# Other order at the beginning and between like operations, in a convolution with quantised weights

## The chip, the cores and the metric

One core of one Trainium2 chip. The metric is the device time of one execution in microseconds (us). The kernel before took 1002.18 us, the median of 3 runs (1001.09 to 1002.53). TensorE is called PE here (PEld is its weight load), VectorE DVE, ScalarE ACT, GpSimd POOL, SyncE SP, as in the profile.

## The reference

The input x has 160 images of 128 channels and 32 x 32 pixels. U holds 5 sets of 128 x 128 x 9 weights; image i belongs to the set i % 5 of the reference's order, and the kernel works through them set by set, 32 images each.

```python
beta, alpha = jnp.max(U), jnp.min(U)
s1 = (beta - alpha) / 3.0
v1 = s1 * floor(U / s1)
s2 = s1 / 5.0
v2 = s2 * floor((U - v1) / s2)
w = (v1 + v2).reshape(128 * 5, 128, 3, 3)
# group norm over 32 groups of 4 channels, no scale or shift
z = (x - mean) / sqrt(var + 1e-5)
out = x + conv(z, w, 3x3, padding 1, 5 groups)
```

## The kernel before

**Weights.** `weight_range` finds the range of all U, `Steps.from_range` makes the two step sizes. `make_column` quantises one column of taps (three kernel rows) in 14 small DVE steps (`floor_div`, L108 to L112, `nearest` L99, L125, L453) that a generator gives out one by one; PE turns the result (L462), ACT writes it as `wt` and `half` (L475, L476), and POOL makes the sum and difference taps from it. The three columns of the first set are made at the start (`first`, `second`, `third`). Those of the next set are taken step by step during the images (`take(later, 1)`), from stage 4 of the first set and from the third image of the others, and what is left is run four images before the set ends.

**Statistics.** `measure` gives the sum (L192) and the sum of squares (L199) of one image on ACT, or both on DVE (`st.image`, L182 to L186) where `by_vector` says so. Images go in groups (`cuts`). When a group is measured, PE averages over the channels (`means`, L208), POOL and ACT make deviations, PE averages again (`variances`, L225), and POOL makes `rstd` and `shift` (L235 to L244). Stage i measures ahead up to i + min(10 + i // 2, 15).

**Parts of an image.** A *direct* image (all even ones, and 1, 3, 5) is normalised to z (ACT, L510), rounded to f16 as `hi` (ACT, L518), and the rest of z is `lo` (DVE, L573). From `lo`, `combinations` makes `rows`: differences and sums of pixel rows (L587, L589, L590). A *combined* image (odd, from 7) is combined first (`outer_rows` on POOL, `combine` on DVE, L549 to L555) and then split into `vh` (ACT, L560) and `vl` (DVE, L566).

**Products.** Images 0 to 2 run as plain taps (`direct_hi`, `direct_lo`, L613). From image 3 on, two output rows share products. `sums_of_pairs(i)` puts a sum and a difference part into the PSUM tile `m` (one buffer of two banks). `leave(i)` copies half of m away on ACT (L708), and `pairs(i)` adds and subtracts the two into the tile `eo` (two buffers) on DVE (L717, L718). The remaining products of the image go on top of that (`rest_of_column`, L613 and L650). `residual` multiplies eo by 0.5 into `sum` on ACT (L732), and a POOL DMA adds this to x in SBUF (L745); for images 0 to 2 and the last four a DVE operation does it (L737). SP stores and loads two images at a time.

**The order is written by hand.** No planner moves anything: each engine runs its instructions in the order of the program. Before the loop, `run` writes the start out: statistics of images 0 to 3, ten products of zeros (`warm_up`, L631), the first column, parts of images 0 to 2, then plain taps column by column (the middle one first, `COLS = (1, 0, 2)`). Stage i of the loop then puts PE's `conv(i)` first: `sums_of_pairs(i + 1)`, then the rest of image i in three columns, with a waiting group's `means` in front of the second and `variances` in front of the third column. (In stage 3 the sums come with the second column.) With j = i - 1, ACT's order in a stage is

```python
for k in by_scalar: measure(k, (0,))   # L192
residual(j)                            # L732
leave(i + 1)                           # L708
high_combined(i + 3) or normalise(i + 3), high_part(i + 3)
for k in by_scalar: measure(k, (1,))   # L199
```

and DVE's is `low_combined(i + 2)` or `low_part(i + 2)`, one step of `later`, `combinations(i + 2)` for a direct image, `pairs(i + 1)`, then `combine(i + 4)` or another step of `later`, then measuring on DVE. So an odd stage i multiplies a combined image, writes the sums of a direct one, and normalises a direct one.

Of the kernel before, what the change touches and what calls it, by code (L numbers as in the profile page):

```python
# [132 lines left out]
def run(steps):  # L133

    while True:
        try:
            next(steps)
        except StopIteration as end:
            return end.value
# [170 lines left out]
class Main:  # L310
# [24 lines left out]
    STAT_LEAD = 14  # L335
    LOAD_LEAD = 20
    STEADY = 7
    MEASURED = 20
    EARLY = 8
    FIRST = 3  # L340

# [4 lines left out]
    def __init__(self, tc, ctx, keep, x, u, out):  # L346
        nc = self.nc = tc.nc
        self.imgs, C, self.H, self.W = x.shape
        P = self.P = nc.NUM_PARTITIONS
        assert C == P and self.H * self.W == 1024  # L350
        self.per_set = self.imgs // N_SETS
        self.xv = x.rearrange("(b n) c h w -> n c b (h w)", n=N_SETS)
        self.ov = out.rearrange("(b n) c h w -> n c b (h w)", n=N_SETS)
        self.uv = u.rearrange("n (o i k) -> n o i k", o=C, k=TAPS)

        def pool(name, bufs, **kw):
            return ctx.enter_context(tc.tile_pool(name=name, bufs=bufs, **kw))

        self.const = pool("const", 1)
        self.qpool = pool("quant", 1)  # L360
        self.wpool = pool("weights", 2)
        self.upool = pool("u", 1)
        self.xpool = pool("x", 12)
        self.zpool = pool("z", 3)
        self.parts = pool("parts", 5)
        self.rows = pool("rows", 4)
        self.wide = pool("wide", 1)
        self.wide_parts = pool("wide_parts", 2)
        self.evac = pool("evac", 2)
        self.sums = pool("sums", 4)  # L370
        self.unread = pool("unread", 1)
        self.small = pool("small", 3)
        self.ps_eo = pool("ps_eo", 2, space=PSUM)
        self.ps_m = pool("ps_m", 1, space=PSUM)
        self.ps_stat = pool("ps_stat", 1, space=PSUM)
        self.ps_tr = pool("ps_tr", 1, space=PSUM)
        self.steps = Steps(nc, keep)
        self.chunks, self.z, self.hi, self.v, self.eo, self.m = {}, {}, {}, {}, {}, {}
        self.sum = {}
        self.wts = {}  # L380
        self.columns = []

        cuts = [0, 2, 4, 8, 12, *range(16, self.imgs + 1, 8)]
        self.groups = [range(a, b) for a, b in zip(cuts, cuts[1:])]
        self.group_of = {i: k for k, g in enumerate(self.groups) for i in g}
        self.stats = {}
# [95 lines left out]


    def by_vector(self, i):
        return self.EARLY <= i < self.MEASURED and i % 2 == 0

    def measure(self, i, stages=(0, 1)):

# [91 lines left out]
    def combinations(self, i):  # L580


        nc, P, H, W = self.nc, self.P, self.H, self.W
        lo = self.los[i % len(self.los)]
        rows = self.v[i] = self.rows.tile([P, 2048], MM, tag="rows", name=f"rows{i}")
        d, st = self.halves(rows)
        nc.vector.tensor_sub(d, lo[:, 0:H, :], lo[:, 2 : H + 2, :])  # L587
        pairs = lo[:, 1 : H + 1, :].rearrange("p (i a) w -> p a i w", a=2)
        nc.vector.tensor_add(st[:, 0], pairs[:, 0], pairs[:, 1])  # L589
        nc.vector.tensor_sub(st[:, 1], pairs[:, 1], pairs[:, 0])  # L590

    def halves(self, v):

# [28 lines left out]
    def banks(self, pool, tag, i):  # L622
        return pool.tile([self.P, 2, self.H // 2, self.W], F32, tag=tag, name=f"{tag}{i}")

    def warm_up(self):


        zeros = self.los[3].rearrange("p h w -> p (h w)")
        target = self.banks(self.ps_m, "m", "warm")
        for _ in range(10):  # L630
            self.nc.tensor.matmul(  # L631
                target[:, 0].rearrange("p i w -> p (i w)"), zeros[:, :128], zeros[:, :512],
                start=True, stop=True,
            )

    def direct_hi(self, i, col):
# [39 lines left out]
    def conv(self, i, on_the_way):  # L676


        if self.FIRST < i < self.imgs - 1:
            self.sums_of_pairs(i + 1)  # L680

        for halves in ((0,), (1,)) if i == self.imgs - 1 else ((0, 1),):
            for col in self.COLS:
                if col == self.COLS[1] and i == self.FIRST:
                    self.sums_of_pairs(i + 1)
                if col != self.COLS[0] and halves[-1] == 1:
                    on_the_way(col)
                self.rest_of_column(i, col, halves)
        del self.v[i]
# [18 lines left out]
        self.nc.scalar.copy(m2, self.m[i][:, 1])  # L708
        self.m[i] = self.m[i], m2

    def pairs(self, i):

        nc = self.nc
        m, m2 = self.m.pop(i)
        eo = self.eo[i] = self.banks(self.ps_eo, "eo", i)
        rows = eo.rearrange("p h (i a) w -> p (h i) a w", a=2)
        nc.vector.tensor_add(rows[:, :, 0], m[:, 0], m2)  # L717
        nc.vector.tensor_sub(rows[:, :, 1], m[:, 0], m2)  # L718

    def by_hand(self, i):  # L720
# [33 lines left out]
    def run(self):  # L754
# [39 lines left out]
        def take(steps, count):  # L794
            for _ in range(count):
                next(steps, None)
# [29 lines left out]
        measure(1, 3)  # L826
        self.stats[1].means()
        self.stats[1].deviations()
        self.warm_up()
        parts(0)  # L830
        self.stats[1].variances()
        self.stats[1].deviation()
        self.stats[1].scales()
        self.normalise(1)
        run(first)
        self.high_part(1)
        parts(2)
        take(second, 2)
        self.low_part(0)
        take(second, 2)  # L840
        self.low_part(1)
        take(second, 2)
        self.low_part(2)

        for i in range(self.FIRST):
            self.direct_hi(i, self.COLS[0])
# [5 lines left out]
        self.normalise(3)  # L852
        run(second)
        self.high_part(3)
        self.direct_lo(2, self.COLS[0])
        measure(0, 6, 7)
        measure(1, 6, 7)
        for i in range(self.FIRST):
            self.direct_hi(i, self.COLS[1])
            if i == self.FIRST - 1:  # L860
                run(third)
            self.direct_lo(i, self.COLS[1])
        self.stats[2].means()
        self.stats[2].deviations()
        self.low_part(3)
        self.combinations(3)
        self.steps.choose()
        ready, middle, measured, loaded = [], [], self.EARLY, 6
        later, turned = iter(()), []
        for i in range(self.imgs):  # L870
# [27 lines left out]
            else:  # L898
                j = i - 1
                self.conv(i, on_the_way)  # L900
            ahead = i + min(10 + i // 2, self.STAT_LEAD + 1)
            to_measure = range(measured, min(self.imgs, ahead))
            measured += len(to_measure)
            if n + 1 < N_SETS:
                if b == (2 if n == 0 else 0):
                    self.load_set(n + 1)
                if b == (4 if n == 0 else 2):
                    later = (s for col in self.COLS for s in self.make_column(n + 1, col))
            by_scalar = [k for k in to_measure if not self.by_vector(k)]

            if i < self.FIRST:

                if i == self.FIRST - 1:
                    self.leave(i + 1)
                    self.pairs(i + 1)
                    self.combinations(i + 2)
                self.residual(j)
                if i == self.FIRST - 2:
                    self.low_part(i + 3)
                for k in by_scalar:  # L920
                    self.measure(k, (0,))
                self.normalise(i + 4)
                for k in by_scalar:
                    self.measure(k, (1,))
                self.high_part(i + 4)
            else:

                direct = i + 2 < self.imgs and not self.combined(i + 2)
                if self.combined(i + 2):
                    self.low_combined(i + 2)  # L930
                if direct:
                    self.low_part(i + 2)
                take(later, 1)
                if direct:
                    self.combinations(i + 2)
                if i > self.FIRST and self.by_hand(j):
                    self.residual(j)
                for k in by_scalar:
                    self.measure(k, (0,))
                if i > self.FIRST and not self.by_hand(j):  # L940
                    self.residual(j)
                    self.accumulate(j)
                if self.combined(i + 4):
                    self.outer_rows(i + 4)


                if i + 1 < self.imgs:
                    self.leave(i + 1)
                if self.combined(i + 3):
                    self.high_combined(i + 3)  # L950
                elif self.FIRST + 3 < i + 3 < self.imgs:
                    self.normalise(i + 3)
                    self.high_part(i + 3)
                for k in by_scalar:
                    self.measure(k, (1,))
            for st in middle:
# [8 lines left out]
            if i >= self.FIRST:  # L965

                if i + 1 < self.imgs:
                    self.pairs(i + 1)
                if self.combined(i + 4):
                    self.combine(i + 4)  # L970
                else:
                    take(later, 1)
                if b == self.per_set - 4:
                    run(later)

            middle, ready = ready, []
            for k in to_measure:
                if self.by_vector(k):
                    self.measure(k)
                group = self.group_of[k]  # L980
                if k + 1 == self.groups[group].stop:
                    ready.append(self.stats[group])
# [53 lines left out]
```

## Time and profile before

| | us |
|---|---|
| median of 3 runs | 1002.18 |
| the profiled execution | 1001.74 |
| its span | 1000.0 |
| PE busy | 959.1 (96%) |
| ACT busy | 916.5 (92%) |
| DVE busy | 906.7 (91%) |
| POOL busy | 374.4 (37%) |
| PE waits for DVE's L718, in all | 10.5 |
| PE clock granted, 30 to 36 us | 0.50 |

A row of a timeline gives start, duration, engine, line, operation, tiles and shape; in brackets stands how long the engine was idle before it and what ended that. A row of the waits gives who waited for whom, the total in us, how often, and the longest. "L718" is line 718 of the kernel. Matmuls overlap: the spacing of their starts is their price, not the duration of one. The same holds for ACT and DVE to a smaller degree, where a next operation can start some 0.1 us before the row of the last one ends. This spacing of starts is called the pitch.

### The profile page before, as it was taken

The page shows a single profiled execution, that of the slowest core. Times are in us where ns is not written, and L with a number is a line of the kernel's source. Part 1 is how long each engine was busy: PE and PEld are TensorE (multiplying, and loading weights), DVE is VectorE, ACT ScalarE, POOL GpSimd, SP SyncE. Part 2 cuts the span into 40 slices and gives each one's busy share as a digit, 9 for nine tenths or more (in the row PEclk, how much of TensorE's full clock was granted, in tenths as well). Part 3 has the DMA queues.
Part 4 walks back from the last instruction along what each step waited for, and adds up shares of the span by engine and source line. Part 5 has one row for each costly group of instructions (what it writes and reads, how often), then busy time and mean ns, then how long its engine had stood idle before and what let it go on. Part 6 is the DMA issues. An engine that isn't in the chain of part 4 may idle for free.

```text
span 1000.0 us, 15935 instructions
## 1 busy us (share of the span) xinstructions
PE 959.1 (96%) x5920; PEld 576.2 (58%) x5920; DVE 906.7 (91%) x1227; ACT 916.5 (92%) x1249; POOL 374.4 (37%) x567
## 2 busy tenths in 40 slices
PE   1889999999999999999999999999999999999997
PEld 1445556665666665666666566666665666666554
DVE  7989899999999999989999999999999988888884
ACT  4877999999999999999999999999999999998560
POOL 3523164353515143625243443515243523233310
PEclk9899999999999999999999999999999999999999
DMA  9638789999999999999999999999999999997773
GB/s 365 239 105 232 196 220 262 280 262 274 287 272 264 261 273 265 267 275 281 273 279 263 260 270 269 293 276 277 268 253 264 281 282 262 274 244 196 192 179 141
DMA packets 67287, 254.42 MB, mean 254 GB/s; under 512 B 5248, under 2 KB 5248, under 8 KB 67200
## 3 DMA queue, kind: packets, MB, share of 16 engines
q1 hardware_dynamic: 45168, 173.09, 50.5%
q0 software_dynamic: 22032, 80.23, 41.2%
q8 instruction: 48, 0.79, 0.3%
q14 instruction: 39, 0.32, 0.1%
HBM read 89.19 MB, written 83.89 MB: 173 GB/s over the span
## 4 chain that ended last, share of the span: by engine, by line
PE 82%; DVE 8%; ACT 6%; issue 2%; DMA 1%; POOL 1%; SPq 0%; DVEq 0%; ACTq 0%
PE eo L613 27%; PE m L650 27%; PE eo L650 27%; ACT junk L199 2%; ACT vh L560 1%; ACT sum L732 1%; PE m L613 1%; DVE lo L573 1%; DVE eo L717 1%; DVE eo L718 1%; ACT m L708 1%; ACT z L510 1%; DVE vl L566 1%; DVE st L182 1%; DMA range<-in_L_conv_U_dram 1%
## 5 line engine op out<-in xcount | busy, mean ns | idle before, releaser
L650 PEld LDWEIGHTS <-wt 128*128 128x128 f16 x4212 | 410.8, 98 | 238.5 <-DVE eo L718 9.2
L613 PE MATMUL eo<-hi,wt 128*128 128x496 f16 (+1 forms) x1476 | 355.0, 377 | 4.6 <-DVE eo L718 3.3
L745 POOL DMA_DIRECT2D xt<-sum x153 | 135.9, 888 | 456.2 <-ACT sum L732 440.0
L613 PEld LDWEIGHTS <-wt 128*128 128x128 f16 x1548 | 152.1, 100 | 151.1 <-DVE eo L718 3.8
L566 DVE SCALAR_TENSOR_TENSOR vl<-v,rstd,vh 128x2048 f16<-128x2048 f32 x77 | 180.8, 2347 | 3.1 <-ACT vh L560 3.1
L650 PE MATMUL m<-vh,wt 128*128 128x496 f16 (+1 forms) x462 | 175.5, 380 | 5.9 <-DVE eo L718 5.9
L650 PE MATMUL eo<-vl,wt 128*128 128x256 f16 (+1 forms) x924 | 177.1, 273 | 0.0
L650 PE MATMUL eo<-vh,wt 128*128 128x256 f16 (+1 forms) x924 | 177.1, 273 | 0.0
L199 ACT ACTIVATE junk<-xt,mv 128x1024 f16<-128x1024 f32 x154 | 176.3, 1145 | 0.3
L192 ACT ACTIVATE junk<-xt 128x1024 f16<-128x1024 f32 x154 | 162.7, 1057 | 14.0 <-DMA xt<-in_x_dram 10.9
L650 PE MATMUL m<-vl,wt 128*128 128x496 f16 (+1 forms) x462 | 175.4, 380 | 0.0
L732 ACT ACTIVATE sum<-eo 128x1024 f32<-128x1024 f32 x153 | 154.2, 1008 | 16.6 <-PE eo L650 16.6
L717 DVE TENSOR_TENSOR eo<-m,m 128x512 f32<-128x512 f32 x157 | 109.0, 694 | 61.2 <-ACT m L708 60.8
L560 ACT ACTIVATE vh<-v,rstd 128x2048 f16<-128x2048 f32 x77 | 155.0, 2013 | 0.3 <-DVE v L555 0.3
L650 PE MATMUL eo<-rows,wt 128*128 128x248 f16 (+1 forms) x960 | 144.3, 273 | 0.0
L650 PE MATMUL m<-rows,wt 128*128 128x496 f16 (+1 forms) x480 | 116.9, 380 | 1.4 <-DVE eo L718 1.3
L718 DVE TENSOR_TENSOR eo<-m,m 128x512 f32<-128x512 f32 x157 | 109.8, 699 | 5.4
L708 ACT COPY m<-m 128x512 f32<-128x512 f32 x157 | 91.2, 581 | 25.3 <-PE m L650 22.4
L510 ACT ACTIVATE z<-xt,shift,rstd 128x1024 f32<-128x1024 f32 x83 | 103.2, 1244 | 2.6 <-POOL shift L242 2.6
L573 DVE TENSOR_TENSOR lo<-z,hi 128x1024 f16<-128x1024 f32 x83 | 101.6, 1224 | 1.8 <-ACT hi L518 1.8
L518 ACT CAST hi<-z 128x1024 f16<-128x1024 f32 x83 | 86.8, 1045 | 2.5
L549 DVE TENSOR_TENSOR v<-xt 128x960 f32<-128x960 f32 x77 | 88.5, 1150 | 0.0
(111 smaller groups left out, 824.8 us busy)
## 6 DMA issues: line engine op xcount, KB each, us to landing
xt<-in_x_dram SPq DMA_DIRECT2D x78, 1024.0 KB, 8.9
out_dram<-xt SPq DMA_DIRECT2D x78, 1024.0 KB, 5.1
xt<-sum POOLq DMA_DIRECT2D x153, 512.0 KB, 6.8
range<-in_L_conv_U_dram SPq DMA_DIRECT2D x4, 576.0 KB, 7.1
u<-in_L_conv_U_dram SPq DMA_DIRECT2D x4, 576.0 KB, 11.5
xt<-in_x_dram SPq DMA_DIRECT2D x4, 512.0 KB, 10.5
out_dram<-xt SPq DMA_DIRECT2D x3, 512.0 KB, 2.7
u<-in_L_conv_U_dram SPq DMA_DIRECT2D x2, 288.0 KB, 3.1
```

Of the source, the lines that this page charges most:

```text
L192: self.nc.scalar.activation(junk, image, ACTF.Copy, scale=-1.0 / image.shape[1], accum_out=self.mv[:, j, 0:1],)
L199: self.nc.scalar.activation(junk, image, ACTF.Square, bias=self.mv[:, j, 0:1], accum_out=self.mv[:, j, 1:2],)
L510: nc.scalar.activation(z, self.image(i), ACTF.Identity, bias=st.shift[:, j : j + 1], scale=st.rstd[:, j : j + 1],)
L560: self.nc.scalar.mul(vh, self.v[i], st.rstd[:, j])
L566: self.nc.vector.scalar_tensor_tensor(vl, self.v[i], st.rstd[:, j], self.hi[i], ALU.mult, ALU.subtract)
L573: self.nc.vector.tensor_sub(lo[:, 1 : self.H + 1, :].rearrange("p h w -> p (h w)"), self.z.pop(i), self.hi[i].rearrange("p h w -> p (h w)"),)
L613: nc.tensor.matmul(target[:, h, r0 - h0 : r1 - h0, c0:c1], self.wts[n, col][:, k, :], tile[:, s0 : s0 + r1 - r0, c0 + dw : c1 + dw], start ...
L650: self.nc.tensor.matmul(target[:, :, c0:c1], self.wts[n, col][:, kind, :], source[:, :, c0 + dw : c1 + dw], start=start, stop=stop, skip_g ...
L717: nc.vector.tensor_add(rows[:, :, 0], m[:, 0], m2)
L718: nc.vector.tensor_sub(rows[:, :, 1], m[:, 0], m2)
L732: nc.scalar.mul(self.sum[i], eo, 0.5)
L745: self.nc.gpsimd.dma_start(self.image(i), self.sum.pop(i), accum_op=ALU.add)
```

## The change

- The zeros' products become 14 and then 7 more behind the first column of weights.
- Low part 2 moves from before the first plain taps to behind the second column's making; its products with the first column move from before to after the first taps of the second column.
- In stages 0 to 2 the order of measuring, normalising and low parts changes; image 9 has its squares taken two stages later, and `normalise(6)` moves to stage 3. The sums of image 4 come with the third column of image 3, not the second.
- Measuring runs ahead by 10 + i // 4 images, not 10 + i // 2 (15 at most as before). DVE measures images 8, 10, 11, 14, 17, 20, 23, 26 and 29; before, it measured 8, 10, 12, 14, 16 and 18. The group of images 16 to 23 becomes two groups of 4.
- In the loop, `normalise(i + 3)` stands ahead of `leave(i + 1)` and `high_part(i + 3)` behind it.
- `pairs` runs one other DVE step between L717 and L718: the third row step in even stages, a step of `later` in odd ones.

```diff
@@ -335,7 +335,7 @@
     STAT_LEAD = 14
     LOAD_LEAD = 20
     STEADY = 7
-    MEASURED = 20
+    MEASURED = 32
     EARLY = 8
     FIRST = 3
 
@@ -380,7 +380,7 @@
         self.wts = {}
         self.columns = []
 
-        cuts = [0, 2, 4, 8, 12, *range(16, self.imgs + 1, 8)]
+        cuts = [0, 2, 4, 8, 12, 16, 20, *range(24, self.imgs + 1, 8)]
         self.groups = [range(a, b) for a, b in zip(cuts, cuts[1:])]
         self.group_of = {i: k for k, g in enumerate(self.groups) for i in g}
         self.stats = {}
@@ -482,7 +482,7 @@
 
 
     def by_vector(self, i):
-        return self.EARLY <= i < self.MEASURED and i % 2 == 0
+        return i in (8, 10) or self.EARLY <= i < self.MEASURED and i % 3 == 2
 
     def measure(self, i, stages=(0, 1)):
 
@@ -584,10 +584,10 @@
         lo = self.los[i % len(self.los)]
         rows = self.v[i] = self.rows.tile([P, 2048], MM, tag="rows", name=f"rows{i}")
         d, st = self.halves(rows)
-        nc.vector.tensor_sub(d, lo[:, 0:H, :], lo[:, 2 : H + 2, :])
+        yield nc.vector.tensor_sub(d, lo[:, 0:H, :], lo[:, 2 : H + 2, :])
         pairs = lo[:, 1 : H + 1, :].rearrange("p (i a) w -> p a i w", a=2)
-        nc.vector.tensor_add(st[:, 0], pairs[:, 0], pairs[:, 1])
-        nc.vector.tensor_sub(st[:, 1], pairs[:, 1], pairs[:, 0])
+        yield nc.vector.tensor_add(st[:, 0], pairs[:, 0], pairs[:, 1])
+        yield nc.vector.tensor_sub(st[:, 1], pairs[:, 1], pairs[:, 0])
 
     def halves(self, v):
 
@@ -622,15 +622,16 @@
     def banks(self, pool, tag, i):
         return pool.tile([self.P, 2, self.H // 2, self.W], F32, tag=tag, name=f"{tag}{i}")
 
-    def warm_up(self):
+    def warm_up(self, count):
 
 
         zeros = self.los[3].rearrange("p h w -> p (h w)")
-        target = self.banks(self.ps_m, "m", "warm")
-        for _ in range(10):
+        if "warm" not in self.m:
+            self.m["warm"] = self.banks(self.ps_m, "m", "warm")
+        for _ in range(count):
             self.nc.tensor.matmul(
-                target[:, 0].rearrange("p i w -> p (i w)"), zeros[:, :128], zeros[:, :512],
-                start=True, stop=True,
+                self.m["warm"][:, 0].rearrange("p i w -> p (i w)"), zeros[:, :128],
+                zeros[:, :512], start=True, stop=True,
             )
 
     def direct_hi(self, i, col):
@@ -681,7 +682,7 @@
 
         for halves in ((0,), (1,)) if i == self.imgs - 1 else ((0, 1),):
             for col in self.COLS:
-                if col == self.COLS[1] and i == self.FIRST:
+                if col == self.COLS[2] and i == self.FIRST:
                     self.sums_of_pairs(i + 1)
                 if col != self.COLS[0] and halves[-1] == 1:
                     on_the_way(col)
@@ -708,13 +709,15 @@
         self.nc.scalar.copy(m2, self.m[i][:, 1])
         self.m[i] = self.m[i], m2
 
-    def pairs(self, i):
+    def pairs(self, i, between=lambda: None):
+
 
         nc = self.nc
         m, m2 = self.m.pop(i)
         eo = self.eo[i] = self.banks(self.ps_eo, "eo", i)
         rows = eo.rearrange("p h (i a) w -> p (h i) a w", a=2)
         nc.vector.tensor_add(rows[:, :, 0], m[:, 0], m2)
+        between()
         nc.vector.tensor_sub(rows[:, :, 1], m[:, 0], m2)
 
     def by_hand(self, i):
@@ -826,21 +829,20 @@
         measure(1, 3)
         self.stats[1].means()
         self.stats[1].deviations()
-        self.warm_up()
+        self.warm_up(14)
         parts(0)
         self.stats[1].variances()
         self.stats[1].deviation()
         self.stats[1].scales()
         self.normalise(1)
         run(first)
+        self.warm_up(7)
         self.high_part(1)
         parts(2)
         take(second, 2)
         self.low_part(0)
         take(second, 2)
         self.low_part(1)
-        take(second, 2)
-        self.low_part(2)
 
         for i in range(self.FIRST):
             self.direct_hi(i, self.COLS[0])
@@ -852,18 +854,20 @@
         self.normalise(3)
         run(second)
         self.high_part(3)
-        self.direct_lo(2, self.COLS[0])
+        self.low_part(2)
         measure(0, 6, 7)
         measure(1, 6, 7)
         for i in range(self.FIRST):
             self.direct_hi(i, self.COLS[1])
+            if i == 1:
+                self.direct_lo(2, self.COLS[0])
             if i == self.FIRST - 1:
                 run(third)
             self.direct_lo(i, self.COLS[1])
         self.stats[2].means()
         self.stats[2].deviations()
         self.low_part(3)
-        self.combinations(3)
+        run(self.combinations(3))
         self.steps.choose()
         ready, middle, measured, loaded = [], [], self.EARLY, 6
         later, turned = iter(()), []
@@ -898,7 +902,7 @@
             else:
                 j = i - 1
                 self.conv(i, on_the_way)
-            ahead = i + min(10 + i // 2, self.STAT_LEAD + 1)
+            ahead = i + min(10 + i // 4, self.STAT_LEAD + 1)
             to_measure = range(measured, min(self.imgs, ahead))
             measured += len(to_measure)
             if n + 1 < N_SETS:
@@ -907,32 +911,35 @@
                 if b == (4 if n == 0 else 2):
                     later = (s for col in self.COLS for s in self.make_column(n + 1, col))
             by_scalar = [k for k in to_measure if not self.by_vector(k)]
+            by_vector = [k for k in to_measure if self.by_vector(k)]
 
             if i < self.FIRST:
 
-                if i == self.FIRST - 1:
-                    self.leave(i + 1)
-                    self.pairs(i + 1)
-                    self.combinations(i + 2)
+                if i == 0:
+                    measure(0, *by_vector, 9)
+                    self.normalise(4)
+                    self.high_part(4)
+                if i == 2:
+                    self.leave(3)
+                    self.normalise(5)
+                    measure(1, 9)
+                    self.high_part(5)
+                    self.pairs(3)
+                    self.low_part(4)
+                    run(self.combinations(4))
                 self.residual(j)
-                if i == self.FIRST - 2:
-                    self.low_part(i + 3)
-                for k in by_scalar:
-                    self.measure(k, (0,))
-                self.normalise(i + 4)
-                for k in by_scalar:
-                    self.measure(k, (1,))
-                self.high_part(i + 4)
+                if i > 0:
+                    measure(0, *by_vector)
             else:
 
-                direct = i + 2 < self.imgs and not self.combined(i + 2)
+                rows = iter(())
                 if self.combined(i + 2):
                     self.low_combined(i + 2)
-                if direct:
+                elif i + 2 < self.imgs:
                     self.low_part(i + 2)
-                take(later, 1)
-                if direct:
-                    self.combinations(i + 2)
+                    take(later, 1)
+                    rows = self.combinations(i + 2)
+                    take(rows, 2)
                 if i > self.FIRST and self.by_hand(j):
                     self.residual(j)
                 for k in by_scalar:
@@ -944,13 +951,15 @@
                     self.outer_rows(i + 4)
 
 
+                part = i + 3 < self.imgs and not self.combined(i + 3)
+                if part:
+                    self.normalise(i + 3)
                 if i + 1 < self.imgs:
                     self.leave(i + 1)
+                if part:
+                    self.high_part(i + 3)
                 if self.combined(i + 3):
                     self.high_combined(i + 3)
-                elif self.FIRST + 3 < i + 3 < self.imgs:
-                    self.normalise(i + 3)
-                    self.high_part(i + 3)
                 for k in by_scalar:
                     self.measure(k, (1,))
             for st in middle:
@@ -965,7 +974,8 @@
             if i >= self.FIRST:
 
                 if i + 1 < self.imgs:
-                    self.pairs(i + 1)
+                    self.pairs(i + 1, lambda: take(rows if i % 2 == 0 else later, 1))
+                run(rows)
                 if self.combined(i + 4):
                     self.combine(i + 4)
                 else:
@@ -974,9 +984,9 @@
                     run(later)
 
             middle, ready = ready, []
+            if i >= self.FIRST:
+                measure(0, *by_vector)
             for k in to_measure:
-                if self.by_vector(k):
-                    self.measure(k)
                 group = self.group_of[k]
                 if k + 1 == self.groups[group].stop:
                     ready.append(self.stats[group])
```

## The prediction

> **What bounds the kernel now.** I read the table of engines first, then the busy time by stretches, then who waits for whom, then the timeline of one steady pair of images.
>
> ```profile
> PE 959.1 (96%) x5920; PEld 576.2 (58%) x5920; DVE 906.7 (91%) x1227; ACT 916.5 (92%) x1249; POOL 374.4 (37%) x567
> ...
> 300.00:400.00 100.00, 100.00 (x629) 60.86 (x628) 95.34 (x128) 98.93 (x136) 38.34 (x60) 1.00 0.99 266
> ```
>
> PE is busy 959 of 1000 us, and from 300 to 400 us (second line: PE, PEld, DVE, ACT, POOL busy) 100 of 100, with ACT at 98.9. So after the beginning only PE counts, and what the change can win is PE's idle time: 41 us, of which 17.9 pass before its first product and some 7 after its last. The waits of PE:
>
> ```profile
> PE m L650 <- DVE eo L718: 7.2, 5, 2.0
> ...
> PE eo L613 <- DVE eo L718: 3.3, 1, 3.3
> ```
>
> These 10.5 us (at 59, 69, 95, 121, 147 and 231 us) are the prize. All are waits for the second half of `pairs`. Now one odd (combined) image in the steady state:
>
> ```profile
> 509.52 1.46 PE L650 MATMUL m<-rows,wt 128*128 128x512 f16 x6
> 513.45 0.38 PE L650 MATMUL m<-vh,wt 128*128 128x512 f16 x1
> ...
> 510.38 1.01 ACT L732 ACTIVATE sum<-eo 128x1024 f32<-128x1024 f32 x1
> 511.29 0.58 ACT L708 COPY m<-m 128x512 f32<-128x512 f32 x1
> 511.75 1.25 ACT L510 ACTIVATE z<-xt,shift,rstd 128x1024 f32<-128x1024 f32 x1
> 513.04 1.04 ACT L518 CAST hi<-z 128x1024 f16<-128x1024 f32 x1
> ...
> 510.60 0.60 DVE L110 SCALAR_TENSOR_TENSOR tt<-tt,s1r,nn 128x384 f32<-128x384 f32 x1
> 511.90 0.70 DVE L717 TENSOR_TENSOR eo<-m,m 128x512 f32<-128x512 f32 x1 [0.69 <-ACT m L708]
> 512.63 0.70 DVE L718 TENSOR_TENSOR eo<-m,m 128x512 f32<-128x512 f32 x1
> ```
>
> PE starts the sums of the next image at 509.52 (call it T0) and, 3.93 us later, the sums of the one after. Those write the only m buffer, so they need L718 to be over: 512.63 + 0.70 = 513.33, 0.12 us before PE arrives at 513.45. **There is almost no slack here**, though PE never waits. From the rows: the copy L708 starts at 511.29, L717 0.61 later, L718 0.73 later, and PE can go on 0.76 after that, as its waits show (the row below at 148.49, for an L718 at 147.73). So the next sums start no earlier than copy + 2.10 us.
>
> ```profile
> 148.49 0.39 PE L650 MATMUL m<-vh,wt 128*128 128x512 f16 x1 [1.30 <-DVE eo L718]
> ```
>
> The copy comes behind `sum` (L732) in ACT's order, and `sum` reads the eo whose last product ends after T0. Where ACT waited for it, it started 0.20 us after PE's next sums could have started (69.17, against 68.53 + 4 x 0.109 = 68.97). So the copy must start by T0 + 3.93 - 2.10 = T0 + 1.83. Today it can: the sums are done at about T0 + 1.5, `sum` lets ACT go at T0 + 0.2 + 0.91 = T0 + 1.11.
>
> **The change, part by part.**
>
> *Zeros.* The clock is 0.50 from 29.7 to 36.5 us; 14 of the first 18 weight products there are 0.43 apart instead of 0.21, so warm ones save 14 x 0.21 = 3.0 us. 11 more zeros cost 4 x 0.21 before the wait for POOL at 28.34 (hidden by it: the ten end at 27.18) and 7 x 0.21 from 28.95 to 30.45, just as the first weights (L475) come; nothing on the path. But what is late next is ACT:
>
> ```profile
> 39.85 1.23 ACT L510 ACTIVATE z<-xt,shift,rstd 128x1024 f32<-128x1024 f32 x1
> 40.99 0.47 ACT L475 ACTIVATE wt<-pt 128x384 f16<-128x384 f32 x1
> ```
>
> The second column of weights is written at 40.99 because ACT is in one unbroken row of statistics and normalising from 32.3 us, none of which is moved. PE stood at this wait already (41.51). So I cost the zeros at nothing. If the clock turned late and all 14 took 0.43, they would end at 29.5, 1.2 us past the wait that hides them, and the second statistics with them; that is the bound on the other side. The Trainium skill (TensorE: Matmul & The Clock Gate, Part 1) says the clock doubles after about 3.4 us of busy window and falls after an idle one; the rows agree (0.50 for 6.8 us), and by the rule alone the change would win the 3.0 us.
>
> *Low part 2, its products and its place.* Six products (1.27 us) go from before this wait into the stretch after it, where PE has no idle time until 59 us: +1.27 there. The 1.22 us on DVE only changes its place.
>
> *Images 0 to 2.* `measure(8)` now fills DVE's wait at 50.5, low part 4 comes after `pairs(3)`. Adding rows: residual(0) ends at 57.7, measure(10) takes 1.68, so L717 starts at 59.4, L718 at 60.1, and image 3 starts at 60.9 instead of 62.4: -1.5 us.
>
> *A new wait.* Image 11 is now measured on DVE (11 % 3 is 2), behind `pairs(3)` (1.34), low part 4 (1.23), three row steps (1.28), a residual (1.14) and its own 1.75: ready at 66.15. The group's means product stands in PE's order behind image 3's first column, at 62.6. Everything of PE is queued behind it: +3.6 us. With `leave(4)` after sums moved one column on, image 4's stage begins at 71.65 (70.43 today): +1.2.
>
> *Lead and measuring.* ACT gets 9 images instead of 12 up to stage 11 (2.4 us each), which removes ACT's lateness behind the 1.92, 2.03 and 1.30 us stalls in stages 7, 11 and 15. DVE gets 17, 20, 23, 26, 29 later (1.69 each), of which I take 0.45 each into PE by the DVE slack of about 1.2 in that stage (bounds 0 and 1.69).
>
> *Normalise ahead of leave; a step between L717 and L718.* These hold for the whole run. `normalise(i+3)` exists for odd i only (i+3 is even, not combined): exactly the tight stage. It is one ACT instruction, no DMA. The copy now starts at T0 + 0.20 + 0.91 + 1.15 (z's pitch to an independent follower, 54.75 to 55.90) = T0 + 2.26, past the 1.83. Between L717 and L718 comes one step of the next set's weights: L717's pitch is then 0.61 (as L718 to L549: 512.63 to 513.24), the step's on average 0.47 (0.27 to 0.67 by rows), instead of 0.73: +0.35. So the next sums start at T0 + 2.26 + 0.61 + 0.61 + 0.47 + 0.76 = T0 + 4.71, PE waits 4.71 - 3.93 = **0.78 us per pair**; where no set is being prepared, T0 + 2.26 + 2.10 = 4.36, **0.43 us**. In even stages PE's rest is 5.1 us long and all this is hidden. The gains of this edit are hidden too: z to hi 1.29 to 1.15 on ACT, 0.12 on DVE. [...]
>
> **The sum**, against the profiled execution (1001.74 us, span 1000.0; 0.44 under the median shown). Up to stage 7: +1.1 (the +1.2 of image 4, carried on). Stages 7 to 18: six odd stages x 0.78 + 5 x 0.45 - 5.25 (today's stalls), so +2.8 in all at stage 19. From stage 19 to 155 there are 69 odd stages; 44 of them have weight steps (5 in the first set, 13 in each of three): 44 x 0.78 = 34.3; 25 x 0.43 = 10.8. Today's stall at 231 goes: -0.6. At stage 21 normalise(24) may wait for POOL's shift, one stage after its statistics (POOL's L235 took 2.98): +1.5 (0 to 3). Statistics and turn products, some 0.15 each, that PE does inside the new waits: -3.3. Together +45.5: **1047 us**.
>
> **Rivals.**
> *Faster.* PE keeps its 100% because ACT, with 7 us less to do early, runs ahead, so that in odd stages the copy starts by T0 + 1.83. Then only the stalls at 95, 121, 147 and 231 go: -5.9, 996 us. For it: these stalls are ACT's and DVE's lateness, and both get relief. Against: `sum` cannot start before the product it reads, however early ACT is. It decides at 0.43 us.
> *Half the price.* The step between falls beside something, and every odd stage costs 0.43: 69 x 0.43 = 30 and +0.1 for the rest: 1032. For it: in four of ten odd stages that is the case already.
> *Twice the price.* ACT does not come back to T0 + 0.20 but stays 0.66 late as at 510.38: 44 x 1.44 + 25 x 1.09 = 91: 1092. For it: ACT is 98.9% busy. Against: the pair gets 0.78 longer and ACT's work doesn't.
> *No effect.* Costs and gains cancel, if the copy lands at 1.83 by shorter pitches.
>
> **How the numbers follow.** Forecast (1036 to 1058, by pitches 0.15 either way over 69 stages and the early bounds) 0.74; half the price 0.10; twice 0.06; faster 0.08; no effect 0.02. Range 1026 to 1062: forecast and half price, 0.84. A measurement tells about 0.2% from no change; slower by more than that 0.90, within it 0.02, faster 0.08.
>
> **What would show it.** Right: PE's table has "PE m L650 <- DVE eo L718" some 70 times with 0.4 to 0.8 us; PE below 96% at 300 to 400; in an odd stage ACT's order is sum, z, m, hi, sum follows a PE wait. The zeros: clock 1.00 at 30 to 36 us and a wait for L475 at 41.5 that is longer (39.0 to 41.5). The new wait: L208 waits for image 11's statistics near 62 to 66 us. Wrong: if PE is at 100% after 300 us, the odd stage was misread and the start alone decides.

## The result, and the profile after

The changed kernel takes **1050.26 us** (median of 6 runs, 1048.43 to 1051.16) where the kernel before took 1001.65 beside it: a ratio of 1.0482, 95% interval 1.0469 to 1.0496. The prediction was 1047 us in a range of 1026 to 1062. The profiled execution took 1050.74 us, its span is 1049.0.

The table of engines and the stretch from 300 to 400 us (busy us of PE, PEld, DVE, ACT, POOL) of the changed kernel:

```profile
PE 977.0 (93%) x5935; PEld 573.0 (55%) x5935; DVE 896.0 (85%) x1242; ACT 910.9 (87%) x1239; POOL 404.0 (39%) x575
...
300.00:400.00 100.00, 95.58 (x594) 56.79 (x592) 87.75 (x120) 93.84 (x129) 42.18 (x56) 1.00 0.94 255
```

The stretch carries it: 594 matmuls in 100 us, against 629 before, and no engine is full any more. All of PE, DVE and ACT have idle time at once, so this is a chain from engine to engine and not an engine's load. The waits of PE, over the whole run:

```profile
PE m L651 <- DVE eo L721: 34.9, 70, 2.8
...
PE pg L208 <- DVE mv L186: 3.5, 1, 3.5
PE eo L613 <- ACT wt L475: 2.6, 1, 2.6
```

(L651, L719, L721, L709 and L735 are the kernel before's L650, L717, L718, L708 and L732.) In this row, 70 waits for the second half of `pairs` have taken the place of 5. One odd stage, image for image the one shown for the kernel before, from the timelines of PE, ACT and DVE:

```profile
536.00 0.60 PE L651 MATMUL m<-rows,wt 128*128 128x512 f16 x2
540.74 0.39 PE L651 MATMUL m<-vh,wt 128*128 128x512 f16 x1 [0.65 <-DVE eo L721]
...
536.20 1.02 ACT L735 ACTIVATE sum<-eo 128x1024 f32<-128x1024 f32 x1 [0.15 <-PE eo L651]
537.12 1.23 ACT L510 ACTIVATE z<-xt,shift,rstd 128x1024 f32<-128x1024 f32 x1
538.25 0.57 ACT L709 COPY m<-m 128x512 f32<-128x512 f32 x1
538.72 1.05 ACT L518 CAST hi<-z 128x1024 f16<-128x1024 f32 x1
...
538.86 0.70 DVE L719 TENSOR_TENSOR eo<-m,m 128x512 f32<-128x512 f32 x1 [1.02 <-ACT m L709]
539.47 0.61 DVE L110 SCALAR_TENSOR_TENSOR tt<-tt,s1r,nn 128x384 f32<-128x384 f32 x1
540.00 0.69 DVE L721 TENSOR_TENSOR eo<-m,m 128x512 f32<-128x512 f32 x1
```

T0 is 536.00. `sum` now waits for PE and starts at T0 + 0.20; z stands between it and the copy, which starts at T0 + 2.25; L719 follows 0.61 later, the weight step L110 0.61 after that, L721 0.53 after that, and PE goes on 0.74 later, at T0 + 4.74. Before it was T0 + 3.93.

Stage by stage (the start of `sums_of_pairs`, from PE's timeline):

| stretch | before, us | after, us | difference | the prediction's |
|---|---|---|---|---|
| up to stage 4 | 70.4 | 75.8 | +5.4 | +1.2 |
| stages 4 to 18 | 97.6 | 96.6 | -1.0 | +1.6 |
| stages 19 to the end's last sums | 814.5 | 859.1 | +44.6 | +42.7 |

### The profile page after: what moved, and what is told of

Same layout as the page of the kernel before. It is cut to its first block, busy times and chain, and to the rows that moved or that the text cites. A ratio compares the mean times of both kernels' runs of the same rounds, so it can differ in the third digit from the quotient of the medians.

```text
span 1049.0 us, 15983 instructions
## 1 busy us (share of the span) xinstructions
PE 977.0 (93%) x5935; PEld 573.0 (55%) x5935; DVE 896.0 (85%) x1242; ACT 910.9 (87%) x1239; POOL 404.0 (39%) x575
## 4 chain that ended last, share of the span: by engine, by line
PE 57%; ACT 21%; DVE 18%; issue 2%; POOL 1%; DMA 1%; SPq 0%; DVEq 0%; POOLq 0%
PE eo L613 27%; PE m L651 19%; PE eo L651 10%; ACT z L510 7%; ACT sum L735 7%; DVE eo L719 5%; DVE eo L721 5%; ACT m L709 4%; ACT junk L199 1%; DVE vl L566 1%; ACT vh L560 1%; ACT junk L192 1%; PE m L613 1%; DMA range<-in_L_conv_U_dram 1%; DVE st L182 1%
## 5 line engine op out<-in xcount | busy, mean ns | idle before, releaser
L651 PEld LDWEIGHTS <-wt 128*128 128x128 f16 x4212 | 406.4, 98 | 286.8 <-DVE eo L721 57.8
L719 DVE TENSOR_TENSOR eo<-m,m 128x512 f32<-128x512 f32 x157 | 109.0, 694 | 126.2 <-ACT m L709 126.1
L651 PE MATMUL m<-vh,wt 128*128 128x496 f16 (+1 forms) x462 | 177.1, 383 | 34.8 <-DVE eo L721 34.0
L735 ACT ACTIVATE sum<-eo 128x1024 f32<-128x1024 f32 x153 | 155.7, 1018 | 39.8 <-PE eo L651 39.8
L651 PE MATMUL eo<-vl,wt 128*128 128x256 f16 (+1 forms) x924 | 177.1, 273 | 0.0
L651 PE MATMUL eo<-vh,wt 128*128 128x256 f16 (+1 forms) x924 | 177.1, 273 | 0.0
L651 PE MATMUL m<-vl,wt 128*128 128x496 f16 (+1 forms) x462 | 176.4, 382 | 0.0
L199 ACT ACTIVATE junk<-xt,mv 128x1024 f16<-128x1024 f32 x151 | 173.3, 1147 | 0.3
L192 ACT ACTIVATE junk<-xt 128x1024 f16<-128x1024 f32 x151 | 159.8, 1058 | 14.7 <-DMA xt<-in_x_dram 11.6
L651 PE MATMUL eo<-rows,wt 128*128 128x248 f16 (+1 forms) x960 | 144.8, 274 | 0.0
L709 ACT COPY m<-m 128x512 f32<-128x512 f32 x157 | 91.3, 581 | 55.0 <-PE m L651 53.2
L651 PE MATMUL m<-rows,wt 128*128 128x496 f16 (+1 forms) x480 | 117.7, 382 | 0.9 <-DVE eo L721 0.8
L721 DVE TENSOR_TENSOR eo<-m,m 128x512 f32<-128x512 f32 x157 | 108.6, 691 | 1.0
```

What stands on the lines that cost most here:

```text
L192: self.nc.scalar.activation(junk, image, ACTF.Copy, scale=-1.0 / image.shape[1], accum_out=self.mv[:, j, 0:1],)
L199: self.nc.scalar.activation(junk, image, ACTF.Square, bias=self.mv[:, j, 0:1], accum_out=self.mv[:, j, 1:2],)
L651: self.nc.tensor.matmul(target[:, :, c0:c1], self.wts[n, col][:, kind, :], source[:, :, c0 + dw : c1 + dw], start=start, stop=stop, skip_g ...
L735: nc.scalar.mul(self.sum[i], eo, 0.5)
```

## The experiments

Each kernel was timed in turns with the kernel before on the same chip; the kernel before gave 1002.0 to 1002.6 us in these.

**Which edits cost it.** Four kernels divide the change. `start_only` is the changed kernel with

```diff
-                if part:
-                    self.normalise(i + 3)
                 if i + 1 < self.imgs:
                     self.leave(i + 1)
                 if part:
+                    self.normalise(i + 3)
                     self.high_part(i + 3)
...
-                    self.pairs(i + 1, lambda: take(rows if i % 2 == 0 else later, 1))
+                    self.pairs(i + 1)
```

and the steps of `rows` and `later` back in front of `pairs`.

> The changed kernel with the two edits of the steady stages undone: normalise stands behind leave again, and nothing stands between L717 and L718. Theory (the order in odd stages holds PE): the odd stages are 3.93 us again, so 1004 us (999 to 1010): the start's own cost of some 5 us less the early stalls. Rival (the new measuring and lead leave ACT and DVE late for the whole run): most of the 48 us stays, over 1030.

Measured: 1007.82 us (ratio 1.0050, 1.0036 to 1.0063). About 5 of the 48 us belong to all the other edits together. In the profiled execution (1005.56 us, one of the shorter ones) few of them are the start's: from PE's first product to stage 4 it takes 1.3 us more than the kernel before, stages 4 to 18 take 1.3 less, and stages 19 to 30 take 2.2 more (1.7 of it in stage 21); 0.8 us is a later first product. The rival that ACT and DVE stay late for the whole run falls: from stage 31 on the odd stages take 3.92 to 4.24 us again (once 4.78), as in the kernel before (3.92 to 4.23).

`norm_only` is the kernel before with normalise ahead of leave, as in the first diff read backwards; `step_only` is the kernel before with the step between alone; `steady_only` has both.

> The kernel before with one edit: normalise(i + 3) ahead of leave(i + 1). Theory: odd stages of 4.35 us in place of 3.93 to 4.07 over the whole run, 1029 us (1024 to 1036). Rival (the step between alone is to blame): within 3 us of the kernel before. Rival (the start is to blame): the same.

> The kernel before with one edit: another DVE step between the two halves of pairs. Theory: the copy still starts at T0 + 1.52 to 1.8, so only the longer steps stick out, by up to 0.2 us in some stages: 1006 us (1002 to 1012). Rival (the step between alone is to blame): 1030 and more.

> The kernel before with both edits of the steady stages and its own start. Theory: 50 odd stages x 0.78 and 25 x 0.42, less today's stalls: 1044 us (1038 to 1052). If the two add up, this is norm_only and step_only together less 1002; the theory has it above that sum, since the step sticks out fully only behind the later copy.

| kernel | median, us | ratio | interval | odd stages from 31 on, us |
|---|---|---|---|---|
| norm_only | 1028.67 | 1.0261 | 1.0243 to 1.0278 | 4.34 to 4.36, once 4.47 |
| step_only | 1007.49 | 1.0049 | 1.0032 to 1.0065 | 3.92 to 4.27, once 4.88 |
| steady_only | 1046.91 | 1.0443 | 1.0426 to 1.0460 | 4.35 to 4.87 |
| changed kernel | 1050.26 | 1.0482 | 1.0469 to 1.0496 | 4.35 to 4.87 |

All three came as the theory had them. Alone, normalise costs 26 us and the step 5; together they cost 44, 13 more than the sum. That fits the reason given beforehand, that the step's length sticks out fully only where the copy is already late. With the 5 of the other edits this is the whole change. How norm_only looks on ACT, in a stage with T0 = 510.69:

```profile
510.89 1.02 ACT L732 ACTIVATE sum<-eo 128x1024 f32<-128x1024 f32 x1 [0.47 <-PE eo L650]
511.81 1.23 ACT L510 ACTIVATE z<-xt,shift,rstd 128x1024 f32<-128x1024 f32 x1
512.94 0.57 ACT L708 COPY m<-m 128x512 f32<-128x512 f32 x1
```

The copy is at T0 + 2.25 and ACT idles in front of `sum`: it has time, but in the wrong place.

**A double dose.** `norm_hi_ahead` is the kernel before with (`part` is true for the same images as the `elif` of before)

```diff
+                if part:
+                    self.normalise(i + 3)
+                    self.high_part(i + 3)
                 if i + 1 < self.imgs:
                     self.leave(i + 1)
...
-                elif self.FIRST + 3 < i + 3 < self.imgs:
-                    self.normalise(i + 3)
-                    self.high_part(i + 3)
```

> A double dose: the kernel before with normalise(i + 3) and high_part(i + 3) both ahead of leave(i + 1). ACT does the same work. Theory: the copy starts at T0 + 0.20 + 0.91 + 1.28 + 0.95 = T0 + 3.34, the next sums 2.10 later, so odd stages of 5.44 us and 1110 us (1100 to 1116). Rival (a swap on ACT costs what it costs in pipe gaps, not in the place of the copy): about what normalise alone cost, 1025 to 1035.

Measured: 1109.10 us (1.1065, 1.1048 to 1.1082). Every odd stage from 15 to 155 takes 5.43 to 5.45 us; the theory says 5.44. ACT and PE, T0 = 544.24:

```profile
544.45 1.02 ACT L732 ACTIVATE sum<-eo 128x1024 f32<-128x1024 f32 x1 [0.47 <-PE eo L650]
545.37 1.23 ACT L510 ACTIVATE z<-xt,shift,rstd 128x1024 f32<-128x1024 f32 x1
546.63 1.04 ACT L518 CAST hi<-z 128x1024 f16<-128x1024 f32 x1
547.58 0.58 ACT L708 COPY m<-m 128x512 f32<-128x512 f32 x1
...
549.68 0.39 PE L650 MATMUL m<-vh,wt 128*128 128x512 f16 x1 [1.04 <-DVE eo L718]
```

Copy at T0 + 3.34, next sums 2.10 later. With the same work on ACT, 107 us hang on the place of one 0.58 us copy.

**The other side of sum.** `norm_ahead_of_sum` moves normalise one place further up.

```diff
+                if part:
+                    self.normalise(i + 3)
                 if i > self.FIRST and not self.by_hand(j):
                     self.residual(j)
...
-                elif self.FIRST + 3 < i + 3 < self.imgs:
-                    self.normalise(i + 3)
+                elif part:
                     self.high_part(i + 3)
```

> The kernel before with normalise(i + 3) one place further up still, ahead of sum as well. It is then done while ACT waits for the product, and no longer between sum and the copy. Theory: odd stages of 3.93 us again, 1001 us (999 to 1004), since z to hi also costs ACT 0.13 us less per pair. Rival (any normalise ahead of leave costs its 1.15 us): 1028 as with normalise between sum and leave.

Measured: 1005.41 us (1.0033, 1.0022 to 1.0044): 4 us worse than forecast, but not the 1028 of the rival. The stretch from 300 to 400 us is full again:

```profile
300.00:400.00 100.00, 99.99 (x631) 60.65 (x629) 95.07 (x128) 98.27 (x137) 45.40 (x59) 1.00 0.99 270
```

Most of what stays is in stages 9 and 13 (5.19 and 6.12 us where the kernel before has 4.06 and 4.09). In stage 9 ACT comes late from measuring and waits for nobody, and z in front of the copy delays it further. In stage 13 it is z that has to wait, for POOL's shift, and `sum` and the copy stand behind it:

```profile
133.07 1.24 ACT L510 ACTIVATE z<-xt,shift,rstd 128x1024 f32<-128x1024 f32 x1 [2.23 <-POOL shift L242]
```

So "ahead of sum" is free only for an ACT that waits at sum and has its shift already. `lead_and_norm`, the same on top of `lead_only` below, asked whether less early measuring cures that.

> lead_only with normalise(i + 3) ahead of sum. Ahead of sum it made 1005.4 of 1002.0, by odd stages up to 17 in which ACT was late already; from then on the odd stages were 3.92. Theory: with the slower lead ACT is less late, so at most half of the 3.4 us remains: 1001.5 us (1000 to 1003). Rival (normalise ahead of leave costs for good): 1004 and more.

Measured: 1003.25 us (1.0009, 0.9997 to 1.0021), 2.5 above lead_only: a little over the forecast's range; early stages are still paid (5.19 and 5.91 us in stages 13 and 15, against 4.67 and 5.21 in lead_only). No version with normalise ahead of leave paid.

**The zeros.** `zeros_only` is the kernel before with

```diff
-        self.warm_up()
+        self.warm_up(14)
...
         run(first)
+        self.warm_up(7)
```

> The kernel before with 14 and 7 products of zeros in place of 10. Theory: the clock stays at 1.00 from 30 to 36 us, and PE waits longer for the second column's weights at 41.5, so 1002 us (1000.5 to 1003). Rival (the rule of the clock gate alone): the 3.0 us are won, 999.

Measured: 1001.94 us (0.9999, 0.9990 to 1.0008). The clock does stay up; the last column but two of these rows is the granted clock, from 30 to 36 us, first in the kernel before, then in zeros_only:

```profile
30.00:32.00 2.00, 1.51 (x4) 0.58 (x5) 1.97 (x3) 1.75 (x4) 1.92 (x2) 0.50 1.03 412
32.00:34.00 2.00, 2.00 (x6) 0.76 (x5) 1.97 (x4) 1.68 (x2) 1.92 (x4) 0.50 1.02 406
34.00:36.00 2.00, 2.00 (x7) 0.70 (x5) 1.73 (x2) 1.97 (x4) 2.00 (x3) 0.50 1.03 412
```

```profile
30.00:32.00 2.00, 2.00 (x11) 0.89 (x10) 1.70 (x4) 2.00 (x4) 1.84 (x5) 1.00 1.02 406
32.00:34.00 2.00, 1.21 (x7) 0.48 (x5) 1.96 (x4) 1.97 (x3) 2.00 (x3) 1.00 1.04 414
34.00:36.00 2.00, 2.00 (x12) 0.89 (x10) 1.97 (x4) 1.97 (x5) 0.45 (x1) 1.00 1.02 408
```

and the 3 us are given back, most of them in waits for hi of image 2 (0.8), for the second column's k (1.0) and for its L475 (some 0.3), which ACT reaches when it did before, and 0.6 because the first plain tap comes later, 13.2 us behind PE's first product and not 12.6. The fourteen zeros make that delay:

```profile
22.53 5.72 PE L633 MATMUL mwarm<-lo 128*128 128x512 f16 x14
28.55 1.67 PE L633 MATMUL mwarm<-lo 128*128 128x512 f16 x7
```

They take 5.55 us up to the next product, 0.40 each, where the seven later ones lie 0.23 apart. So most of them run at the slow pace, although the clock in this profile reads 1.00 from 16 to 39 us: that reading does not show the slow pace there. The clock stays up afterwards, as forecast, and that is worth nothing here.

**The start.** `start_11_act` and `start_lo2_back` each take one wait out of start_only.

```diff
-        return i in (8, 10) or self.EARLY <= i < self.MEASURED and i % 3 == 2
+        return i in (8, 10) or 12 <= i < self.MEASURED and i % 3 == 2
...
-                    measure(1, 9)
+                    measure(0, 11)
+                    measure(1, 9, 11)
```

> start_only (the new start without the edits of the steady stages) with image 11 measured on ACT, which idles there, not on DVE. Theory: PE's means product no longer waits 3.5 us for DVE: 1004 us (1002 to 1006), against 1007.8 of start_only. If the clock's fall behind this wait costs too, the gain is up to 5 us. Rival (the wait was covered by the later wait for the copy of image 4): under 1 us of gain.

Measured: 1002.19 us (1.0003, 0.9994 to 1.0012): 5.6 below start_only by the medians, 4.7 by the ratios, the most that the forecast allowed. From PE's first product to stage 4 it takes 50.6 us, 1.9 less than the kernel before; stages 19 to 30 take 2.2 more and give that back. `start_only` waits for this image with the whole of PE's queue behind it:

```profile
66.97 0.35 PE L208 MATMUL pg<-mv,gavg 128*128 128x4 f32 x2 [3.48 <-DVE mv L186]
```

`start_lo2_back` puts `low_part(2)` and `direct_lo(2, COLS[0])` back to their old lines.

> start_only with low part 2 and its six products back in their old places. Theory: the products fill PE's 2.6 us wait for the second column again and no longer stand in the full stretch behind it: 1.3 us less than start_only, 1006.5 us, and more where the wait of 2.6 us let the clock fall. Rival (PE's later wait of 3.5 us for image 11 takes all of it back): no change, 1007.8.

Measured: 1005.98 us (1.0038, 1.0024 to 1.0052). The direction is right (-1.8), but the interval overlaps that of start_only, whose runs spread from 1004.3 to 1009.2; this one is not settled. Its profiled execution has a fall of the clock behind the 3.5 us wait for image 11 that it keeps.

`lead_only` is the kernel before with only

```diff
-    MEASURED = 20
+    MEASURED = 32
...
-        cuts = [0, 2, 4, 8, 12, *range(16, self.imgs + 1, 8)]
+        cuts = [*range(0, 4, 2), *range(4, 32, 4), *range(32, self.imgs + 1, 8)]
...
-        return self.EARLY <= i < self.MEASURED and i % 2 == 0
+        return i in (8, 10) or 12 <= i < self.MEASURED and i % 4 == 2
...
-            ahead = i + min(10 + i // 2, self.STAT_LEAD + 1)
+            ahead = i + min(10 + i // 4, self.STAT_LEAD + 1)
```

> The kernel before with the slower lead alone: 10 + i // 4, groups of 4 up to image 31, DVE measures 8, 10, 14, 18, 22, 26 and 30. Image 11 stays on ACT, so PE's means product waits for nobody new. Theory: the stalls of stages 7, 11 and 15 (5.25 us) and at 231 us (0.6) go, at most: 997 us (996 to 1000). Rival (DVE's queue was late there, not ACT's): 1000 to 1003.

Measured: 1000.74 us (0.9987, 0.9978 to 0.9996). Faster, but 3.7 short of the forecast, and inside the range of the rival that DVE's queue was late. From 75 us on, the kernel before, then lead_only:

```profile
PE m L650 <- DVE eo L718: 5.9, 4, 2.0
```

```profile
PE m L650 <- DVE eo L718: 3.9, 6, 1.1
```

The stalls of stages 7 and 11 went (4.06 and 3.93 us in place of 6.01 and 6.26), that of stage 15 hardly (5.21 for 5.39), that of stage 29 not at all (4.86 for 4.88), and smaller ones came in stages 9, 13, 19 and 21 (4.6 to 5.1 us). The traces show both engines behind them. L717 follows the copy by 0.61 us where it waits for it; in stages 9, 15 and 19 of lead_only it follows by 1.6 to 2.2 us, as DVE is still at other work (stage 15 below). In stages 13 and 21 ACT is late: `sum` starts 1.7 and 2.1 us after T0, behind a measurement.

```profile
140.57 0.58 ACT L708 COPY m<-m 128x512 f32<-128x512 f32 x1 [0.27 <-PE m L650]
142.79 0.69 DVE L717 TENSOR_TENSOR eo<-m,m 128x512 f32<-128x512 f32 x1
```

Stage 7 of the kernel before was DVE's as well, and not ACT's as the prediction has it: ACT itself waits for PE there, and L717 comes 3.0 us after the copy.

```profile
93.15 0.59 ACT L708 COPY m<-m 128x512 f32<-128x512 f32 x1 [0.52 <-PE m L650]
96.18 0.69 DVE L717 TENSOR_TENSOR eo<-m,m 128x512 f32<-128x512 f32 x1
```

Only 2.0 of the 5.9 us were won for good.

`start_mended` joins several of these: start_11_act with image 11's sum taken in stage 0, low part 2 in its old place, the sums of image 4 with the second column again, and lead_only's groups and by_vector.

> The new start with its own waits removed: image 11 on ACT (its sum in stage 0, its squares in stage 2), low part 2 in its old place, the sums of image 4 with the second column again, groups of 4 up to image 31 and DVE measuring 8, 10, 14, 18, 22, 26 and 30; the steady stages as in the kernel before. Theory: the stalls at 59 and 69 us (4.6) go or shrink beside those that lead_only takes: 997 us (995 to 1000). Rival (another wait of the start takes their place): 1000 and more.

Measured: **997.42 us** (0.9957, 0.9943 to 0.9970), 4.6 us faster than the kernel before it was timed with, and some 53 less than the changed one takes. In its profile, PE's first product to stage 4 takes 3.6 us less than in the kernel before, stages 4 to 18 take 3.1 less and stages 19 to 30 take 2.1 more; which of the joined edits makes how much of that was not tried. Its first 75 us have no wait of PE for DVE's pairs over 0.5 us, where the kernel before had 3.3 and 1.3:

```profile
PE pg L225 <- POOL dv L222: 2.5, 2, 2.1
PE pt L462 <- DVE k L112: 1.5, 1, 1.5
PE m L613 <- ACT hi L518: 0.8, 1, 0.8
PE eo L613 <- DVE eo L721: 0.5, 1, 0.5
PE m L651 <- DVE eo L721: 0.3, 1, 0.3
```

## Why the prediction was right

**The odd stage: right, in mechanism and in size.** Forecast 4.36 us without a weight step, measured 4.34 or 4.35 in 24 of 25 (stage 29 took 5.08); with a step 4.71 on average, measured 4.48 to 4.87, mean 4.69 (stages from 23 on). The rival "faster" fails where the prediction said it would: `sum` starts at T0 + 0.20 and not sooner, with ACT idle ahead of it. "Half the price" and "twice the price" fail by the means; ACT came back to T0 + 0.20, as its idle time shows (at `sum` it waits for PE 77 times, 39.8 us in all; before, 9 times and 16.6 us).

**The new wait for image 11: right** (3.5 us where 3.6 were forecast), and so was the worth of the zeros (nothing). The reading beside it, that the rows agree with a fall of the clock behind an idle window, does not hold: in the 3.4 us before the fall at 29.7 us PE had waited 1.15 us once and was some 0.5 us into its next wait.

**Stage 21: in its bounds.** It took 6.91 us, some 2.2 over the stages around it, where 1.5 (0 to 3) were given for a wait for POOL. That wait is about half of it; the rest is `sum`, which starts 1.44 us after T0 (184.98), behind a measurement.

```profile
188.53 1.24 ACT L510 ACTIVATE z<-xt,shift,rstd 128x1024 f32<-128x1024 f32 x1 [1.10 <-POOL shift L242]
```

The stall at 231 us (stage 29), which the sum lets go for -0.6, stayed: 4.88 us before, 4.87 in start_only, 5.08 in the changed kernel.

**The start: too cheap by 4.2 us.** What failed is that the sum up to image 4 had no price for the clock. In the profiled execution it was down at 42.3 to 45.7 and at 69.6 to 73.0 us, behind the very waits (2.6 and 3.5 us) that the change makes or lengthens; the products there took 1.7 us more each time, and this execution began 0.7 later. The rest of that sum was right, as start_only shows: its profiled execution has the same two waits and no fall of the clock. Stage 4 begins so in the kernel before, start_only and the changed kernel:

```profile
70.43 1.47 PE L650 MATMUL m<-rows,wt 128*128 128x512 f16 x6 [1.29 <-DVE eo L718]
72.49 1.47 PE L651 MATMUL m<-rows,wt 128*128 128x512 f16 x6 [0.43 <-DVE eo L721]
75.81 1.47 PE L651 MATMUL m<-rows,wt 128*128 128x512 f16 x6 [0.43 <-DVE eo L721]
```

Counted from PE's first product (at 17.89, 18.68 and 18.61 us) these are 52.5, 53.8 and 57.2 us: +1.3 without the falls of the clock, where +1.2 was forecast. The last column but two of these rows is the granted clock in the changed kernel:

```profile
42.00:44.00 2.00, 1.76 (x5) 0.70 (x6) 1.82 (x4) 2.00 (x4) 1.28 (x3) 0.58 0.03 8
44.00:46.00 2.00, 2.00 (x7) 0.68 (x5) 1.89 (x4) 1.94 (x5) 1.31 (x2) 0.56 0.55 145
```

**Stages 4 to 18: too dear by 2.6 us.** Two terms were mis-sized, in opposite directions. The relief of ACT and the extra measuring were to give -3.0 together (-5.25 and 5 x 0.45); in start_only, which has both and not the steady edits, these stages take 96.3 us against 97.6, so only -1.3. The steady edits were to cost 6 x 0.78 = 4.7 there; from start_only to the changed kernel these stages grow by 0.3, and the six odd ones (7 to 17) take 28.1 us in both. They were longer than 3.93 us already (4.06 to 5.20 in start_only), so the price of an undisturbed stage did not come on top. The changed kernel enters stage 4 later, which may help it here; that was not tried.

**The sum** was 45.5 us over the kernel before's own profiled time; the profiled execution after was 49.0 over it. Of the 3.5 missing, 4.2 are the start's, -2.6 the next stages', 1.9 the rest, most of it the clock after stage 21 (stage 22 takes 9.41 us for 7.72). So the total came closer than its parts did: the errors of the first two partly cancel, and that is luck.

## What to carry to other kernels

Where an in-order engine both waits for a product and then frees a buffer that the next products need, the distance between these two of its instructions is part of the loop; find the stage with the least slack and add up its pitches (the spacings of starts) before putting anything in between. A full PE says nothing about that slack: it was 0.12 us here with PE at 100%. Work put ahead of the wait is free only once that engine does wait there, and only if that work has nothing to wait for itself.

## What the runs showed of the hardware

**PE's clock falls after waits of 2 to 3.5 us, in some executions and not in others.** In the profile of zeros_only a wait of 2.0 us ends at 122.5, and the clock is at 0.50 from about 123.3 to 126.7; stage 12 takes 9.55 us in place of 7.86. The kernel before has the same wait (2.03 us, to 123.4) without that. In steady_only the products run at the slow pace right behind a wait of 2.5 us that ends at 137.8; stage 14 takes 9.36 us in place of 7.72. In the changed kernel the wait of 2.8 us in stage 21 has the same end:

```profile
190.00:192.00 2.00, 0.11 (x1) 0.11 (x2) 1.73 (x4) 2.00 (x3) 0.30 (x2) 1.00 0.97 248
192.00:194.00 2.00, 2.00 (x7) 0.79 (x7) 2.00 (x3) 1.97 (x5) 0.00 (x0) 0.63 1.07 311
194.00:196.00 2.00, 2.00 (x7) 0.64 (x6) 2.00 (x4) 0.42 (x1) 0.89 (x1) 0.52 1.00 252
```

Here, at both falls of the changed kernel's start and in zeros_only the clock was down for 3.4 us and the fall cost some 1.7 us. The profile of start_only has waits of 2.6 and 3.5 us and no fall. That fits the spread of its runs (4.9 us) beside that of start_mended (1.3), whose longest wait behind the zeros is 1.5 us. The mean granted clock of start_only's ten runs goes with it: 0.998 in the three shortest (1004.3 to 1005.6 us), 0.993 to 0.995 in the four longest (1008.7 to 1009.2). No run tried the falls by themselves.

**A wait of PE looks shorter in the table of waits than it is.** In norm_only most late odd stages are 0.42 us longer, and from stage 19 on the kernel takes 26.0 us more; the table of waits gives 12.4 us in 44 waits from 190 us on, 0.28 each. A likely reason is that the ends of matmuls in the profile are modelled: the shown end of the last one lies behind the start that the next one could have had. PE's busy time of the changed kernel, 18 us higher with 15 products more, fits this; the three falls of the clock can explain only some 5 us of it. The spacing of starts is the safer measure.
